# An attention and mixture-of-experts layer on one core: the experts' inner channels as stationary weights, and an empty unit in the planner

## The chip, the core and the metric

The kernel runs on one core of a Trainium2 chip, all in float32. The core has five engines that run beside each other: TensorE (PE in the profile; its weight loads are PEld), VectorE (DVE), ScalarE (ACT), GpSimd (POOL) and SyncE (SP), which here only issues DMAs. The metric is the device time of one execution in microseconds.

## The reference

The input x is 4 x 1024 tokens of 256 channels, treated here as 4096 rows. With xn the layer norm of x, the result is x + attention(xn) + ffn(xn).

The attention part is a causal linear attention of 16 heads of 16 channels, mixed per head with what four memory banks give for the queries. The ffn part is a mixture of experts:

```
scores = softmax(xn @ gate_weight.T)            # 8 experts
cw     = the 2 largest per token, normalized, else 0
g      = silu(xn @ w_gate[e].T) * (xn @ w_up[e].T)   # 176 inner channels
y      = sum over e of cw[e] * (g @ w_down[e].T)
y     += the same with a shared expert of 352 inner channels
```

The change touches the line of g for the eight routed experts.

## The kernel before

Tokens are handled in 8 blocks of 512 (four tiles of 128). A prologue normalizes all blocks, stores xn to DRAM (`xns`), copies x to DRAM (`sums`), and picks two experts for every token. A counting sort then gives every (token, expert) pair a slot: the slots form 71 tiles of 128, each tile belonging to one expert (`owner`). `islot` holds the token of each slot, and `wslot` its weight.

After that come 32 attention rounds, one per token tile (`attention_round`). Each round's list of units names scores (L723), masks (L730), memories (L838, L848 to L867), local attention (L749), its normalization (`back`, L765 to L789) and the state update. `odd_keys(n + 1)` (L710, on ACT) closes round n: it makes `skO`, a masked copy of the next tile's keys `skT`, which the next round's `scores` needs (L723).

Beside the rounds run the projections. `projections(blk)` makes the keys of block blk and the queries of block blk+1 (`project`, L632, then `projected`, L646 and L650, on DVE), and for blocks 3, 4 and 5 the shared expert too. They are divided by weight over the four rounds of the block before blk. Blocks 2, 6 and 7 have no shared part there, so they have at most four pairs of units; with four pairs, the queries stand first and the keys last. For even blocks, `batch_weights` (L672 to L696: a small softmax on DVE and ACT whose result `w5` the batch's rounds need) stands at their end.

The routed experts are a third stream. For slot tile j:

- `fetch_rows(j)`: an indirect DMA by POOL gathers the 128 rows of xn into `xg`.
- `fetch_weights(j)`: SP reads the owner and loads `wgu` (gate and up weights, 256 x 2 x 176) and `wdn` (down weights, 176 x 256, as 88 partitions x 2). Three buffers each.
- `expert_turn(j)`: turns the hidden values of tile j (two transposes, L1071) and the gathered rows of tile j+2 (two transposes, L1075), and copies all four from PSUM (L1077, ACT).
- `expert_hidden(j)`: two matmuls (the two halves of the 256 input channels) with the turned rows as stationary operand and 352 weight columns moving (L1084). Tokens come out on the partitions. tanh (L1089, ACT) and two DVE passes of 176 columns (L1090, L1091) form silu(gate) * up in a tile `hidden`.
- `expert_out(j)`: two matmuls of 88 rows each (L1097), scaled by `wslot` on ACT (L1101).
- `put(j)`: an indirect DMA by POOL adds the rows to `sums` (L1106).

In the stream, `experts()` orders them: hidden(j), put(j-2), out(j-1), turn(j). The order on every engine is the order in which units are recorded. Each unit has a hand-written weight; `mix` interleaves streams by their relative progress in weight, and `split` divides a stream into parts. The experts fill rounds 2 to 29 up to a common level of weight:

```
share = [weight(rounds[n]) + weight(beside[n]) for n in range(first_round, last_round)]
level = max(share)
cap = 1.25 * weight(work) / len(share)
```

where `weight` leaves out units without arguments. All matmul outputs but the scores rotate through four PSUM banks (`bank`), so a unit needs that the fourth unit before it has been read out. In the last rounds the outputs and `sums` are added and stored.

Of the kernel before, what the change touches and what calls it, by code (L numbers as in the profile page):

```python
# [8 lines left out]
FP = mybir.dt.float32  # L9
I32 = mybir.dt.int32  # L10
AF = mybir.ActivationFunctionType
ALU = mybir.AluOpType
AX = mybir.AxisListType

P = 128
# [7 lines left out]
def linear_attention_moe_kernel(  # L23
# [28 lines left out]
    nc = tc.nc  # L52
    T, H = x.shape
# [3 lines left out]
    NC = H // P  # L57
    HC = NH // NC
    NG = HC // 2
    NM = memories.shape[1]  # L60
    D1 = HD + 1
    CW = 32
    FR = E * F
    FT = w_gate.shape[1]
    FS = FT - FR
    NF = -(-FS // P)
    FH = F // 2
    assert FH * 2 == F and FH <= P and NC == 2 and NM == 4
    HID = eg_w1.shape[1]
    NBLK = T // TB  # L70
    NTT = T // P
# [1 line left out]
    NST = 2 * NTT + E - 1  # L73
# [7 lines left out]
    const = ctx.enter_context(tc.tile_pool(name="const", bufs=1))  # L81
# [5 lines left out]
    exw = ctx.enter_context(tc.tile_pool(name="exw", bufs=3))  # L87
    exp = ctx.enter_context(tc.tile_pool(name="exp", bufs=2))
    dram = ctx.enter_context(tc.tile_pool(name="dram", bufs=1, space=bass.MemoryType.DRAM))
# [5 lines left out]
    st = {}  # L95
    def bank(name):
        return ps_r.tile([P, 512], FP, tag="r", name=name)
# [76 lines left out]

    xns = dram.tile([T + P, H], FP, tag="xns", name="xns")
    sums = dram.tile([T + P, H], FP, tag="sums", name="sums")
    ident = const.tile([P, P], FP, tag="ident", name="ident")
    make_identity(nc, ident)
    ones = const.tile([P, P], FP, tag="ones", name="ones")
# [64 lines left out]
    mem = const.tile([P, NC, KM], FP, tag="mem", name="mem")  # L244
    normx = const.tile([P, NC, NM, HC], FP, tag="normx", name="normx")
    alive = const.tile([P, NMN], FP, tag="alive", name="alive")

    hidden = [const.tile([P, FH + P], FP, tag=f"hidden{k}", name=f"hidden{k}") for k in range(2)]
    for t in hidden:
        nc.gpsimd.memset(t[:, F:], 0.0)  # L250
    ungate = const.tile([P, NH], FP, tag="ungate", name="ungate")
    gates = const.tile([P, H], FP, tag="gates", name="gates")

# [780 lines left out]
    def fetch_rows(j):  # L1034
        if j >= NST:
            return
        xg = exp.tile([P, H], FP, tag="xg", name=f"xg_{j}", bufs=3)
        nc.gpsimd.indirect_dma_start(  # L1038
            out=xg,
            out_offset=None,  # L1040
            in_=xns,
            in_offset=bass.IndirectOffsetOnAxis(ap=islot[:, j : j + 1], axis=0),
        )
        st["xg", j] = xg

    def fetch_weights(j):
        if j >= NST:
            return
        e = nc.sync.value_load(owner[0:1, j : j + 1], min_val=0, max_val=(E - 1) * F)
        wgu = exw.tile([P, NC, 2, F], FP, tag="wgu", name=f"wgu_{j}")  # L1050
        for g, w in enumerate((w_gate, w_up)):
            nc.sync.dma_start(
                wgu[:, :, g, :],
                w[:, bass.ds(e, F)].rearrange("(k p) f -> p k f", p=P),
            )
        wdn = exw.tile([FH, 2, H], FP, tag="wdn", name=f"wdn_{j}")
        nc.sync.dma_start(
            wdn, w_down[bass.ds(e, F), :].rearrange("(f p) h -> p f h", p=FH)
        )
        st["weights", j] = wgu, wdn  # L1060

    def expert_turn(j):


        fetch_rows(j + 4)
        fetch_weights(j + 3)
        pt = bank(f"pte_{j}").rearrange("p (f t) -> p f t", t=P)
        lo, hi = (0 if j >= 0 else 2), (4 if j + 2 < NST else 2)
        if j >= 0:
            for f in range(2):  # L1070
                nc.tensor.transpose(pt[:, f, :], hidden[j % 2][:, f * FH : f * FH + P], ident)  # L1071
        if j + 2 < NST:
            xg = st.pop(("xg", j + 2))
            for c in range(NC):
                nc.tensor.transpose(pt[:, 2 + c, :], xg[:, c * P : (c + 1) * P], ident)  # L1075
        dst = exp.tile([P, 4, P], FP, tag="turned", name=f"turned_{j}")
        nc.scalar.copy(dst[:, lo:hi], pt[:, lo:hi])  # L1077
        st["hTe", j], st["xgT", j + 2] = dst[:, 0:2], dst[:, 2:4]

    def expert_hidden(j):  # L1080
        xgT, wgu = st.pop(("xgT", j)), st["weights", j][0]
        ph = bank(f"phe_{j}")
        for k in range(NC):
            nc.tensor.matmul(  # L1084
                ph[:, : 2 * F], xgT[:, k, :], wgu[:, k].rearrange("p g f -> p (g f)"),
                start=(k == 0), stop=(k == NC - 1),
            )
        th = hidden[j % 2][:, :F]
        nc.scalar.activation(th, ph[:, :F], AF.Tanh, scale=0.5)  # L1089
        nc.vector.scalar_tensor_tensor(th, th, 1.0, ph[:, :F], ALU.add, ALU.mult)  # L1090
        nc.vector.scalar_tensor_tensor(th, th, 0.5, ph[:, F : 2 * F], ALU.mult, ALU.mult)  # L1091

    def expert_out(j):
        hT, wdn = st.pop(("hTe", j)), st.pop(("weights", j))[1]
        py = bank(f"pye_{j}")
        for f in range(2):
            nc.tensor.matmul(  # L1097
                py[:, :H], hT[:FH, f, :], wdn[:, f, :], start=(f == 0), stop=(f == 1)
            )
        y = exp.tile([P, H], FP, tag="y", name=f"y_{j}", bufs=3)  # L1100
        nc.scalar.activation(y, py[:, :H], AF.Copy, scale=wslot[:, j : j + 1])  # L1101
        st["y", j] = y
# [25 lines left out]
    def run(units):  # L1128
        for _, f, *args in units:
            f(*args)  # L1130

    def late(pairs):

        units = [pairs[0][0]]
        for (_, b), (a, _) in zip(pairs, pairs[1:]):
            units += [a, b]
        return units + [pairs[-1][1]]

    def keys(blk):
        return [  # L1140
            ((1024, project, blk, wk, c, False), (64, projected, blk, c, False))
            for c in range(NC)
        ]

    def queries(blk):
        return [
            ((1024, project, blk, wq, c, True), (64, projected, blk, c, True))
            for c in range(NC)
        ]

    def shared(blk):
        units = []
        for f in range(NF):
            units += [
                ((1024, shared_gate, blk, f), None),
                ((1024, shared_up, blk, f), (64, shared_hidden, blk, f)),
            ]
        return units
# [11 lines left out]
    def projections(blk):  # L1170

        pairs = keys(blk) + (queries(blk + 1) if blk + 1 < NBLK else [])

        pairs += shared(blk) if 2 < blk < NBLK - 2 else []
        if len(pairs) == 4:
            pairs = pairs[2:] + pairs[:2]
        units = [u for pair in pairs for u in pair]
        if blk % BPB == 0:
            b = blk // BPB
            at = units.index(pairs[3 if len(pairs) > 6 else 1][1]) + 1  # L1180
            units[at:at] = [(64, mean_queries, b)]
            at = units.index(pairs[6][0]) if len(pairs) > 6 else len(units)
            units[at:at] = [(64, batch_weights, b)]
        return [u for u in units if u]

    def attention_round(n):

# [17 lines left out]
        return u  # L1205

    def experts():
        units = [(3000, lambda: None), (256, expert_turn, -2), (256, expert_turn, -1)]
        for j in range(NST + 1):
            if j < NST:  # L1210
                units += [(704, expert_hidden, j)]
            units += [(64, put, j - 2)] if j > 1 else []
            units += [(512, expert_out, j - 1)] if j > 0 else []
            units += [(512, expert_turn, j)] if j < NST else []
        return units + [(64, put, NST - 1)]

    def split(units, parts):
# [41 lines left out]
    for blk in range(NBLK):  # L1259
        rows = slice(blk * TB, (blk + 1) * TB)  # L1260
        nc.sync.dma_start(sums[rows, :], x[rows, :])


    def sorting():
# [13 lines left out]
    start = [u for u in late(first_pairs) if u]  # L1278
    start.insert(9, (64, mean_queries, 0))
    start += [(64, batch_weights, 0), (32, odd_keys, 0)]  # L1280
    run(mix(steps(sorting(), 32, 1000), start))


    rounds = [attention_round(n) for n in range(NTT + 2)]
    beside = [[u for pair in shared(blk) for u in pair if u] for blk in (1, 2)] + [[], []]
    for blk in range(2, NBLK):
        beside += split(projections(blk), NT)
# [7 lines left out]
    lists += [(768, add_slots, batches[-2]), (100, hold, batches[-1])]  # L1295
    lists += [(768, add_slots, batches[-1])]
    lists += [(64, inverted), (10, fetch_rows, 0), (10, fetch_rows, 1), (10, fetch_weights, 0)]
    lists = split(lists, first_round)
    for n in range(first_round):
        run(mix(rounds[n], beside[n], lists[n]))  # L1300
# [4 lines left out]
    def weight(units):  # L1305
        return sum(u[0] for u in units if len(u) > 2)

    work = experts()
    share = [weight(rounds[n]) + weight(beside[n]) for n in range(first_round, last_round)]
    level = max(share)  # L1310
# [4 lines left out]
    for n in range(first_round, last_round):  # L1315
        run(mix(*[u for u in (rounds[n], beside[n], side[n - first_round]) if u]))
# [76 lines left out]
```

## Time and profile before

| | |
|---|---|
| median of three runs | 691.95 us (688.85 to 694.77) |
| the profiled execution | 687.07 us, span 685.4 us, mean granted clock 0.99 |
| busy: PE, PEld, DVE | 646.1, 461.9, 454.8 us |
| busy: ACT, POOL | 267.1, 386.8 us |
| DMA | 81.52 MB, mean 119 GB/s |
| expert matmuls phe (L1084), pye (L1097) | 97.5 and 76.7 us of PE busy time |
| expert gathers (L1038), scatters (L1106) | 70.5 and 113.3 us of POOL busy time |

The profile is of one execution, so a sum is made against its 687.07 us, not against the median. Busy times of PE overlap, since matmuls are pipelined: the start of an instruction against the start of the next one is the cost. Each float32 matmul stands in the trace as two instructions with a weight load each, and a transpose as one. A group's line gives busy time and the mean of one in ns, then the idle time of the engine just before it and what ended it. The profile also lists, for any stretch, the clock that was granted to TensorE.

### The profile page before, as it was taken

What the parts mean: (1) busy time and instruction counts of PE and PEld (TensorE: products, weight loads), DVE (VectorE), ACT (ScalarE), POOL (GpSimd) and SP (SyncE); (2) the same over time, 40 slices, a digit from 0 to 9 for tenths busy, and PEclk for the clock granted to TensorE, in tenths of its full rate; (3) what the DMA queues carried; (4) which work ended last, traced back from release to release, by engine and by line L of the source; (5) the groups of instructions that cost most, each with busy time, mean ns of one, the idle gap of its engine ahead of it and who ended that gap; (6) DMA issues with size and microseconds to landing.
All of it is one profiled execution on the core that took longest, in us unless ns stands there. A gap on an engine that the chain in (4) does not pass through costs nothing.

```text
span 685.4 us, 14244 instructions
## 1 busy us (share of the span) xinstructions
PE 646.1 (94%) x5084; PEld 461.9 (67%) x5084; DVE 454.8 (66%) x1198; ACT 267.1 (39%) x614; POOL 386.8 (56%) x424
## 2 busy tenths in 40 slices
PE   4999999899999899999999999999898999999896
PEld 3874565677777666676776767677676776667475
DVE  6838997666666657565756666666676566777672
ACT  3754644334444343334433333334343444334210
POOL 4300254556776735565565555566666567686575
PEclk9999999999999989999999999999999999999999
DMA  9683000436565623344453433345556466563384
GB/s 302 216 279 93 0 1 2 119 91 160 119 145 127 141 64 84 91 100 94 95 103 88 98 95 92 83 112 125 120 124 142 102 145 139 127 149 75 80 282 154
DMA packets 86483, 81.52 MB, mean 119 GB/s; under 512 B 7549, under 2 KB 84013, under 8 KB 86285
## 3 DMA queue, kind: packets, MB, share of 16 engines
q1 hardware_dynamic: 71085, 60.40, 30.6%
q0 software_dynamic: 13632, 18.62, 16.0%
q10 hardware_dynamic: 1696, 1.58, 0.7%
q8 instruction: 41, 0.67, 0.4%
q14 instruction: 29, 0.24, 0.1%
HBM read 62.62 MB, written 22.15 MB: 124 GB/s over the span
## 4 chain that ended last, share of the span: by engine, by line
PE 78%; DVE 14%; ACT 3%; issue 2%; POOL 1%; DMA 1%; DVEq 0%; ACTq 0%
PE phe L1084 13%; PE pye L1097 9%; PE po L990 6%; PE quad L723 5%; PE psu L953 5%; PE pv L396 4%; PE pg L939 4%; PE pn L749 4%; PE po L994 4%; PE quad L838 4%; PE pk L632 3%; PE pq L632 3%; PE pte L1071 2%; PE pt L892 2%; PE pte L1075 2%
## 5 line engine op out<-in xcount | busy, mean ns | idle before, releaser
L1106 POOL DMA_INDIRECT sums<-y,islot x71 | 113.3, 1596 | 70.3 <-DMA sums<-y,islot 18.8
L1084 PE MATMUL phe<-wgu,turned 128*128 128x352 f32 x276 | 97.5, 476 | 3.0 <-ACT turned L1077 2.2
L1090 DVE SCALAR_TENSOR_TENSOR hidden<-hidden,phe 128x176 f32<-128x176 f32 x71 | 23.8, 335 | 95.5 <-ACT hidden L1089 94.9
L730 DVE TENSOR_TENSOR sT<-quad,causal 128x512 f32<-128x512 f32 x128 | 80.5, 683 | 7.5 <-PE quad L723 7.1
L1038 POOL DMA_INDIRECT xg<-xns,islot x71 | 70.5, 993 | 18.7 <-issue 10.8
L1097 PE MATMUL pye<-wdn,turned 88*128 88x256 f32 x284 | 76.7, 393 | 2.5 <-issue 2.4
L860 POOL TENSOR_TENSOR cg<-coarse,gates 128x256 f32<-128x256 f32 x32 | 24.5, 765 | 95.5 <-DVE h L917 59.0
L1084 PEld LDWEIGHTS phe<-wgu,turned 128*128 128x128 f32 x276 | 48.5, 192 | 25.8 <-issue 6.4
L1097 PEld LDWEIGHTS pye<-wdn,turned 88*128 88x128 f32 x284 | 49.8, 190 | 16.4 <-issue 9.9
L1101 ACT ACTIVATE y<-pye,wslot 128x256 f32<-128x256 f32 x71 | 33.6, 473 | 64.0 <-PE pye L1097 64.0
L878 POOL TENSOR_TENSOR fm<-fm 128x512 f32<-128x512 f32 x32 | 44.1, 1379 | 20.0 <-DVE fm L867 12.4
L1077 ACT COPY turned<-pte 128x512 f32<-128x512 f32 (+1 forms) x71 | 41.1, 578 | 34.2 <-PE pte L1075 32.0
L1089 ACT ACTIVATE hidden<-phe 128x176 f32<-128x176 f32 x71 | 22.5, 317 | 78.6 <-PE phe L1084 76.5
L939 PE MATMUL pg<-xnT,wg 128*128 128x512 f32 (+1 forms) x96 | 45.7, 598 | 1.8 <-DVE loc L783 1.8
L990 PE MATMUL po<-wd,h 128*128 128x256 f32 (+1 forms) x192 | 47.2, 382 | 0.1
L953 PE MATMUL psu<-xnT,wu 128*128 128x512 f32 (+1 forms) x96 | 45.6, 597 | 0.0
L590 POOL TENSOR_TENSOR held<-ones,two 128x213 f32<-128x213 f32 (+1 forms) x22 | 15.3, 702 | 48.7 <-DVE ones L570 48.7
L867 DVE TENSOR_TENSOR fm<-quad,rw 128x512 f32<-128x512 f32 x64 | 42.0, 680 | 0.0
L848 DVE TENSOR_SCALAR rw<-quad 128x80 f32<-128x80 f32 x32 | 7.6, 239 | 49.3 <-PE quad L838 49.3
L990 PEld LDWEIGHTS po<-wd,h 128*128 128x128 f32 (+1 forms) x192 | 35.2, 191 | 6.3 <-ACT oc L902 0.8
L928 DVE SCALAR_TENSOR_TENSOR o<-diff,prob,loc 128x256 f32<-128x256 f32 x32 | 35.5, 1109 | 3.9 <-DVE prob L926 0.5
L749 PE MATMUL pn<-sT,va 128*32 128x128 f32 x1024 | 34.6, 276 | 0.3 <-ACT turned L1077 0.3
(210 smaller groups left out, 1389.0 us busy)
## 6 DMA issues: line engine op xcount, KB each, us to landing
wgu<-in_w_gate_dram SPq DMA_DIRECT2D x71, 176.0 KB
wgu<-in_w_up_dram SPq DMA_DIRECT2D x71, 176.0 KB
wdn<-in_w_down_dram SPq DMA_DIRECT2D x71, 176.0 KB
xns<-x SPq DMA_DIRECT2D x8, 512.0 KB
sums<-in_x_dram SPq DMA_DIRECT2D x8, 512.0 KB
x<-in_x_dram SPq DMA_DIRECT2D x7, 512.0 KB
part<-sums SPq DMA_DIRECT2D x12, 256.0 KB
out_dram<-acc SPq DMA_DIRECT2D x12, 256.0 KB
```

The source lines that it names most:

```text
L632: nc.tensor.matmul(pq, w[:, k, c * P : (c + 1) * P], xnT[:, k, :], start=(k == 0), stop=(k == NC - 1),)
L730: nc.vector.tensor_mul(sT, quad[:, g, :].rearrange("p (c t) -> p c t", t=P), causal[:, None, :].to_broadcast([P, NC * 2, P]),)
L749: nc.tensor.matmul(pn[CW * r : CW * (r + 1), q, :], wide[:, i, first : first + CW], st["sT", h // 2][:, c * 2 + h % 2, :], start=True, sto ...
L867: nc.vector.tensor_mul(fm[:, c].rearrange("p g m (r k) -> p g (m r) k", k=HD), quad[:, :, c * KM + KX + KN : (c + 1) * KM].rearrange("p g ...
L878: nc.gpsimd.tensor_add(fm[:, :, 0:2, :], fm[:, :, 0:2, :], fm[:, :, 2:4, :])
L939: nc.tensor.matmul(pg[:n, :], wg[:, k, f * P : f * P + n], xnT[:, k, :], start=(k == 0), stop=(k == NC - 1),)
L953: nc.tensor.matmul(pu[:n, :], wu[:, k, f * P : f * P + n], xnT[:, k, :], start=(k == 0), stop=(k == NC - 1),)
L990: nc.tensor.matmul(po[:, :H], st["h", blk, f][:k, tok], wd[:k, f, :], start=(f == 0), stop=False)
L1038: nc.gpsimd.indirect_dma_start(out=xg, out_offset=None, in_=xns, in_offset=bass.IndirectOffsetOnAxis(ap=islot[:, j : j + 1], axis=0),)
L1084: nc.tensor.matmul(ph[:, : 2 * F], xgT[:, k, :], wgu[:, k].rearrange("p g f -> p (g f)"), start=(k == 0), stop=(k == NC - 1),)
L1097: nc.tensor.matmul(py[:, :H], hT[:FH, f, :], wdn[:, f, :], start=(f == 0), stop=(f == 1))
L1106: nc.gpsimd.indirect_dma_start(out=sums, out_offset=bass.IndirectOffsetOnAxis(ap=islot[:, j : j + 1], axis=0), in_=st.pop(("y", j)), in_of ...
```

## The change

1. **The operands of the hidden matmuls are swapped.** The gate and up weights (in slices of 128, 128 and 112 columns) are stationary, and the 128 turned tokens move. The inner channels come out on the partitions, ready for the down projection, so the hidden values are not transposed any more. Three output slices of one PSUM bank hold: gate 0 to 111 (with 16 rows not used), gate 112 to 175 above up 112 to 175, and up 0 to 111. The tanh and the first DVE pass run over two slices (256 columns); the product with up is two DVE passes of 128 columns, on 112 and on 64 partitions.
2. **Rearranged up weights.** So that the second slice falls as it does, each expert's up channels are rotated in DRAM: two DMAs at the end of the prologue copy w_up to `ups`, and `fetch_weights` reads `ups`. `wdn` is split 112 + 64 and is loaded as 112 partitions x 2 (224 KB in place of 176, its last 48 rows not used).
3. **Order and weights of the expert stream.** `expert_turn(j)` turns only the gathered rows of tile j and stands before `expert_out`; the stream is hidden(j), put(j-2), turn(j+2), out(j-1). Weights: 768 for hidden (704 before), 256 for turn (512 before). The tiles `hidden` and their memset go.
4. **An idle unit.** For blocks with at most four pairs of projections (2, 6 and 7), an empty unit with a third of their weight is put at the end of the list that is divided over four rounds.

```diff
-        for g, w in enumerate((w_gate, w_up)):
+        for g, w in enumerate((w_gate, ups)):
...
-        wdn = exw.tile([FH, 2, H], FP, tag="wdn", name=f"wdn_{j}")
+        wdn = exw.tile([FA, 2, H], FP, tag="wdn", name=f"wdn_{j}")
...
     def expert_turn(j):
-        fetch_rows(j + 4)
-        fetch_weights(j + 3)
-        pt = bank(f"pte_{j}").rearrange("p (f t) -> p f t", t=P)
-        if j >= 0:
-            for f in range(2):
-                nc.tensor.transpose(pt[:, f, :], hidden[j % 2][:, f * FH : f * FH + P], ident)
...
+        fetch_rows(j + 2)
+        fetch_weights(j + 1)
+        xg = st.pop(("xg", j))
+        for c in range(NC):
+            nc.tensor.transpose(pt[:, c, :], xg[:, c * P : (c + 1) * P], ident)
+        xgT = exp.tile([P, NC, P], FP, tag="turned", name=f"turned_{j}")
+        nc.scalar.copy(xgT, pt[:, :NC])
...
     def expert_hidden(j):
-        for k in range(NC):
-            nc.tensor.matmul(
-                ph[:, : 2 * F], xgT[:, k, :], wgu[:, k].rearrange("p g f -> p (g f)"),
-                start=(k == 0), stop=(k == NC - 1),
-            )
-        th = hidden[j % 2][:, :F]
-        nc.scalar.activation(th, ph[:, :F], AF.Tanh, scale=0.5)
-        nc.vector.scalar_tensor_tensor(th, th, 1.0, ph[:, :F], ALU.add, ALU.mult)
-        nc.vector.scalar_tensor_tensor(th, th, 0.5, ph[:, F : 2 * F], ALU.mult, ALU.mult)
+        for s, cols in enumerate((slice(0, P), slice(FA, FA + P), slice(F + FB, 2 * F))):
+            for k in range(NC):
+                nc.tensor.matmul(
+                    ph[: cols.stop - cols.start, s, :],
+                    wgu[:, k].rearrange("p g f -> p (g f)")[:, cols],
+                    xgT[:, k, :],
+                    start=(k == 0), stop=(k == NC - 1),
+                )
+        th = exp.tile([P, 2, P], FP, tag="th", name=f"the_{j}")
+        nc.scalar.activation(th, ph[:, :2], AF.Tanh, scale=0.5)
+        nc.vector.scalar_tensor_tensor(th, th, 1.0, ph[:, :2], ALU.add, ALU.mult)
+        nc.vector.scalar_tensor_tensor(
+            th[:FA, 0], th[:FA, 0], 0.5, ph[:FA, 2], ALU.mult, ALU.mult
+        )
+        nc.vector.scalar_tensor_tensor(
+            th[:FB, 1], th[:FB, 1], 0.5, ph[FB:, 1], ALU.mult, ALU.mult
+        )
...
-        return [u for u in units if u]
+        units = [u for u in units if u]
+        return units + ([] if len(pairs) > 4 else [(sum(u[0] for u in units) // 3, idle)])
...
-            if j < NST:
-                units += [(704, expert_hidden, j)]
+            units += [(768, expert_hidden, j)] if j < NST else []
             units += [(64, put, j - 2)] if j > 1 else []
+            units += [(256, expert_turn, j + 2)] if j + 2 < NST else []
             units += [(512, expert_out, j - 1)] if j > 0 else []
-            units += [(512, expert_turn, j)] if j < NST else []
...
+    for dst, src in ((slice(FB, F), slice(0, FA)), (slice(0, FB), slice(FA, F))):
+        nc.sync.dma_start(
+            ups.rearrange("h (e f) -> h e f", f=F)[:, :, dst],
+            w_up[:, :FR].rearrange("h (e f) -> h e f", f=F)[:, :, src],
+        )
```

with `FB = P // 2` (64), `FA = F - FB` (112), and `idle` a function that does nothing.

More of the change, by code (lines that the diff above doesn't have):

```diff
@@ L66, in linear_attention_moe_kernel @@
     NF = -(-FS // P)
-    FH = F // 2
-    assert FH * 2 == F and FH <= P and NC == 2 and NM == 4
+    FB = P // 2
+    FA = F - FB
+    assert FA <= P and F >= P and NC == 2 and NM == 4
     HID = eg_w1.shape[1]
@@ L176, in linear_attention_moe_kernel @@
     sums = dram.tile([T + P, H], FP, tag="sums", name="sums")
+    ups = dram.tile([H, FR], FP, tag="ups", name="ups")
     ident = const.tile([P, P], FP, tag="ident", name="ident")
@@ L246, in linear_attention_moe_kernel @@
     alive = const.tile([P, NMN], FP, tag="alive", name="alive")
-    hidden = [const.tile([P, FH + P], FP, tag=f"hidden{k}", name=f"hidden{k}") for k in range(2)]
-    for t in hidden:
-        nc.gpsimd.memset(t[:, F:], 0.0)
     ungate = const.tile([P, NH], FP, tag="ungate", name="ungate")
@@ L1055, in fetch_weights @@
             )
-        wdn = exw.tile([FH, 2, H], FP, tag="wdn", name=f"wdn_{j}")
+        wdn = exw.tile([FA, 2, H], FP, tag="wdn", name=f"wdn_{j}")
         nc.sync.dma_start(
-            wdn, w_down[bass.ds(e, F), :].rearrange("(f p) h -> p f h", p=FH)
+            wdn, w_down[bass.ds(e, 2 * FA), :].rearrange("(f p) h -> p f h", p=FA)
         )
@@ L1062, in expert_turn @@
     def expert_turn(j):
-        fetch_rows(j + 4)
-        fetch_weights(j + 3)
-        pt = bank(f"pte_{j}").rearrange("p (f t) -> p f t", t=P)
-        lo, hi = (0 if j >= 0 else 2), (4 if j + 2 < NST else 2)
-        if j >= 0:
-            for f in range(2):
[L1071 to L1075, printed above, removed]
@@ L1076, in expert_turn @@
-        dst = exp.tile([P, 4, P], FP, tag="turned", name=f"turned_{j}")
-        nc.scalar.copy(dst[:, lo:hi], pt[:, lo:hi])
-        st["hTe", j], st["xgT", j + 2] = dst[:, 0:2], dst[:, 2:4]
+        fetch_rows(j + 2)
+        fetch_weights(j + 1)
+        pt = bank(f"pte_{j}").rearrange("p (c t) -> p c t", t=P)
+        xg = st.pop(("xg", j))
+        for c in range(NC):
+            nc.tensor.transpose(pt[:, c, :], xg[:, c * P : (c + 1) * P], ident)
+        xgT = exp.tile([P, NC, P], FP, tag="turned", name=f"turned_{j}")
@@ L1080, in expert_hidden @@
+        nc.scalar.copy(xgT, pt[:, :NC])
+        st["xgT", j] = xgT
     def expert_hidden(j):
         xgT, wgu = st.pop(("xgT", j)), st["weights", j][0]
-        ph = bank(f"phe_{j}")
-        for k in range(NC):
-            nc.tensor.matmul(
-                ph[:, : 2 * F], xgT[:, k, :], wgu[:, k].rearrange("p g f -> p (g f)"),
-                start=(k == 0), stop=(k == NC - 1),
-            )
-        th = hidden[j % 2][:, :F]
-        nc.scalar.activation(th, ph[:, :F], AF.Tanh, scale=0.5)
@@ L1090, in expert_hidden @@
-        nc.vector.scalar_tensor_tensor(th, th, 1.0, ph[:, :F], ALU.add, ALU.mult)
-        nc.vector.scalar_tensor_tensor(th, th, 0.5, ph[:, F : 2 * F], ALU.mult, ALU.mult)
+        ph = bank(f"phe_{j}").rearrange("p (s t) -> p s t", t=P)
+        for s, cols in enumerate((slice(0, P), slice(FA, FA + P), slice(F + FB, 2 * F))):
[6 more added lines that the diff above has]
+                )
@@ L1093, in expert_out @@
+        th = exp.tile([P, 2, P], FP, tag="th", name=f"the_{j}")
[7 more added lines that the diff above has]
+        )
+        st["hTe", j] = th
     def expert_out(j):
@@ L1095, in expert_out @@
         py = bank(f"pye_{j}")
-        for f in range(2):
+        for f, n in enumerate((FA, FB)):
             nc.tensor.matmul(
-                py[:, :H], hT[:FH, f, :], wdn[:, f, :], start=(f == 0), stop=(f == 1)
+                py[:, :H], hT[:n, f, :], wdn[:n, f, :], start=(f == 0), stop=(f == 1)
             )
@@ L1130, in run, with idle @@
             f(*args)
+    def idle(*_):
+        pass
     def late(pairs):
@@ L1207, in experts @@
     def experts():
-        units = [(3000, lambda: None), (256, expert_turn, -2), (256, expert_turn, -1)]
+        units = [(3000, lambda: None), (256, expert_turn, 0), (256, expert_turn, 1)]
         for j in range(NST + 1):
-            if j < NST:
-                units += [(704, expert_hidden, j)]
+            units += [(768, expert_hidden, j)] if j < NST else []
             units += [(64, put, j - 2)] if j > 1 else []
+            units += [(256, expert_turn, j + 2)] if j + 2 < NST else []
             units += [(512, expert_out, j - 1)] if j > 0 else []
-            units += [(512, expert_turn, j)] if j < NST else []
         return units + [(64, put, NST - 1)]
```

## The prediction

> **What bounds the kernel.** I read the page's head and busy row first, then the chain that ended last.
>
> ```profile
> span 685.4 us, 14244 instructions
> PE 646.1 (94%) x5084; PEld 461.9 (67%) x5084; DVE 454.8 (66%) x1198; ACT 267.1 (39%) x614; POOL 386.8 (56%) x424
> PE 78%; DVE 14%; ACT 3%; issue 2%; POOL 1%; DMA 1%; DVEq 0%; ACTq 0%
> ```
>
> TensorE sets the end: it is 94% busy and 78% of the chain. DVE is second, with 231 us idle, but its 14% says that PE now and then runs up against DVE's order. So TensorE time counts nearly in full, DVE time in part, ACT and DMA time not at all unless they come late. Next, the costliest groups, for durations of what is edited:
>
> ```profile
> L1084 PE MATMUL phe<-wgu,turned 128*128 128x352 f32 x276 | 97.5, 476 | 3.0 <-ACT turned L1077 2.2
> L1090 DVE SCALAR_TENSOR_TENSOR hidden<-hidden,phe 128x176 f32<-128x176 f32 x71 | 23.8, 335 | 95.5 <-ACT hidden L1089 94.9
> L867 DVE TENSOR_TENSOR fm<-quad,rw 128x512 f32<-128x512 f32 x64 | 42.0, 680 | 0.0
> L1077 ACT COPY turned<-pte 128x512 f32<-128x512 f32 (+1 forms) x71 | 41.1, 578 | 34.2 <-PE pte L1075 32.0
> ```
>
> A matmul's 476 ns overlaps with its neighbours, so what an instruction costs is the distance from one start to the next. That is read from the timeline (start, length, engine, line); each f32 matmul stands as two instructions, a transpose as one:
>
> ```profile
> 352.82 0.60 PE L800 MATMUL pk<-ident,skT 128*128 128x128 f32 x4
> 353.26 0.38 PE L1071 MATMUL pte<-ident,hidden 128*128 128x128 f32 x2
> 353.48 0.38 PE L1075 MATMUL pte<-ident,xg 128*128 128x128 f32 x2
> 353.70 1.46 PE L990 MATMUL po<-wd,h 128*128 128x256 f32 x6
> ...
> 355.86 1.35 PE L1084 MATMUL phe<-wgu,turned 128*128 128x352 f32 x4
> 357.05 0.53 PE L672 MATMUL pr<-normx,qr 128*128 128x32 f32 x4
> ...
> 363.86 0.63 PE L771 MATMUL pb<-state,sqT 128*128 128x136 f32 x4
> 364.32 1.35 PE L1084 MATMUL phe<-wgu,turned 128*128 128x352 f32 x4
> ```
>
> Four instructions of 352 moving columns take 357.05 - 355.86 = 1.19 us, 0.297 each; a pair of transposes takes 0.22, 0.11 each; four of 136 columns, each with its own 128x128 load, take 0.46, 0.115 each.
>
> Last, where PE waits. Two large waits stand at the first tiles of blocks 2 and 6 (from two timeline windows and the table of windows, whose column after the five engines is the granted clock):
>
> ```profile
> 236.87 0.81 PE L723 MATMUL quad<-sqT,skO 32*128 32x128 f32 x8 [1.89 <-ACT skO L710]
> 529.55 0.68 DVE L650 SCALAR_TENSOR_TENSOR skT<-pk,ek 128x512 f32<-128x512 f32 x1
> 531.52 0.26 ACT L684 ACTIVATE rel<-rel 128x64 f32<-128x64 f32 x1 [4.12 <-DVE rel L683]
> 531.68 0.49 ACT L710 ACTIVATE skO<-skT,own 128x256 f32<-128x256 f32 x1
> 532.23 0.50 PE L723 MATMUL quad<-sqT,skO 32*128 32x128 f32 x8 [2.90 <-ACT skO L710]
> 236.60:243.40 6.80, 6.53 (x34) 4.30 (x35) 3.74 (x14) 1.59 (x4) 4.85 (x5) 0.50 0.43 75
> 533.60:537.00 3.40, 3.40 (x15) 3.03 (x15) 2.73 (x6) 1.55 (x3) 2.05 (x2) 0.50 0.53 100
> ```
>
> The block's keys (skT) leave DVE only as the block's scores begin; the batch weights (rel) follow on DVE and stand ahead of skO on ACT; PE waits 1.9 and 2.9 us for skO. Right after both waits TensorE's clock is halved, for 6.8 and 3.4 us.
>
> **The expert's matmuls.** Removed per tile of slots: 4 instructions of 352 columns, 4 x 0.297 = 1.19 us, and 2 transposes of the hidden values, 0.22: 1.41. Added: three output groups x two contraction halves x two = 12 instructions of 128 columns. Their spacing isn't in the trace for this shape; the nearest rows give 0.11 (transposes of 128 columns) and 0.115 (136 columns, ordinary f32). I take 0.11: 1.32 us. Gain 0.09 us x 71 tiles = **6 us**. Ends: 0.115 gives 2, 0.107 (352 columns' 0.297 scaled to 128) gives 9. The down projection has two matmuls as before, with 112 and 64 rows in place of 88 and 88: nothing.
>
> The rule against this: the Trainium skill, "TensorE: Matmul & The Clock Gate", sections "LDWEIGHTS (loading the stationary operand)" and "Part 3: Packing small matmuls", says that a load costs its columns over 1.2 (107 ns for 128) and overlaps running matmuls only when the row groups differ. All loads here use all rows. By it, loads add up: before 4 x (107 + 297) + 2 x 217 = 2.05 us, after 12 x 217 = 2.60, so +0.55 x 71 = 39 us slower (an estimate from that page). The trace doesn't agree: at 0.297 and 0.115 a load of 190 ns is plainly under the previous matmul, though rows are the same. I follow the row.
>
> **DVE.** From 335 ns at 176 columns to 680 at 512 is 1.03 ns per column. The two passes of 176 (670 ns) become one of 256 (417) and two of 128 (286 each): 989. That is +0.32 us x 71 = 22.6 us more DVE work. Most lies in idle time: DVE waits 94.9 us just ahead of L1090. What stands behind it on DVE is the normalization (L779 to L783), whose PSUM bank PE wants back, and the masks. Bounds: 0 or slightly below (PE's transposes no longer wait for the hidden values; the result isn't needed before the next tile's down projection), and 22.6 if all is in series. DVE being 14% of the chain points to 14% of 22.6; I take **+3 us**.
>
> **ACT, DMA, POOL.** The copy shrinks from 512 to 256 columns (578 to the 370 ns of a 256-column copy, L1000), the tanh grows by 80 columns (65 ns): 10 us less on an engine that is 39% busy, worth nothing. wdn grows from 176 to 224 KB per tile, 3.4 MB on 81.5: SP waits 306.9 us in all for wdn's buffers to be freed, so loads are ahead of use; uncovered, some 3.4 MB at 119 GB/s, 29 us over 16 engines spread over 71 tiles. The rearranged copy of the up weights is two DMAs of 2048 pieces (448 and 256 bytes). q1's 71085 packets took 30.6% of 16 x 685 us, 47 ns each: 4096 pieces on 16 engines make some 12 us. They queue on SP after the copies to sums, issued by 47 us; SP then waits until 124.9, and slices 5 to 7 of the GB/s row show 0, 1 and 2. First use is at 125.5: hidden with over 50 us to spare, else 12 us once. Row gathers and scatters keep their number and order: expert_turn moves ahead of expert_out, but is one iteration lighter; SP meets wdn's wait for the same down projection.
>
> **The idle unit.** Blocks 2, 6 and 7 have only keys and next queries. A third of their weight as empty work at the end puts all of it in the first three of four rounds; expert tiles fill the fourth. In the new order of instructions block 2's keys and the batch weights come about a round (some 17 us) ahead of skO of tile 8; likewise block 6. So both waits go, 1.9 + 2.9 = 4.8 us, and nothing is left on skO but its own 0.5 us on ACT. Half clock for 6.8 and 3.4 us loses half of that: 5.1. Here a second rule weighs: the same page, section "Why this matters for your kernels", asks for PE gaps over about 3 us before the clock falls back. By it only the second wait, of 2.9, could be the cause, and I could claim 1.7. The trace has the halving after 1.9 us as well (but none after a wait of 2.4 at 490.7), each time at once after the gap; I take **9.9 us** in all, 6.5 by the rule.
>
> **Sum.** On the profiled execution, 687.07 us (span 685.4 and 1.7 around it): -6 - 9.9 + 3 = -13, or 674. The three runs before have their median at 691.95, 4.9 above the profiled one; with the same offset the time is **679 us**.
>
> **Rivals.**
> - DVE becomes the bound: the three passes come due in series, +22.6 in place of 3. 691.95 - 15.9 + 22.6 = 699 us. For it: POOL slows DVE (an o pass of 1.88 us at 490.05 ended in a PE wait of 2.4). Against: a third of DVE's time is idle. Slower than before from 16 of the 22.6 us exposed. Chance 0.09.
> - Weight loads show: by the rule above 691.95 + 39 - 9.9 + 3 = 724 us. It decides from a spacing of 0.125 us on (12 x 0.125 = 1.50, +0.09 x 71 = 6.4, what the rest gains). Against: 0.115 in the trace. Chance 0.06.
> - The waits move rather than go: the denser third of the block or the filled fourth round leaves PE waiting elsewhere, and the clock falls there. 691.95 - 6 + 3 = 689 us. For it: PE is idle 39 us in many small places. Chance 0.11.
>
> The forecast itself has 0.74. About 1% is what a measurement of this kernel tells from no change: faster than 685 has 0.75 (the forecast, and a little of the third rival), within 1% 0.16 (most of the third rival and half of the first, whose 699 lies on the border), slower 0.09. The range, 667 to 690, goes from all bounds at their good end (9 for the matmuls, 2 gained on DVE: 671, and an offset smaller by 4) to the third rival.
>
> **What will show it.** Right: phe with 852 instructions near 276 ns of which 12 take 1.3 us; one pair of transposes per tile; DVE busy near 477 us; no wait of quad for skO over 0.5 us; no half clock near 240 and 530 us; span near 672. Wrong: a spacing over 0.12, new PE waits on DVE lines L779 to L783 or on the hidden passes, or a halved clock at another place.

## The result: 3.4% slower

The changed kernel takes 715.51 us (median of 4 runs, 710.77 to 717.47) against 690.4 for the kernel before in the same comparison: a ratio of 1.0344, with a 95% interval of 1.027 to 1.0417. That is some 24 us more where 13 less were forecast. The median of the kernel before differed between comparisons (686.5 to 690.4), so differences below are taken between ratios; a point is 0.01 of a ratio, 6.9 us. Ratios leave out executions more than 1.5% above the fastest of their kernel: two of e4's four (744.22, the profiled one, and 743.19, against 735.04 and 731.91) and two of e9's 22.

The page of the changed kernel (span 715.8 us), its busy row and chain:

```profile
PE 669.3 (94%) x5510; PEld 484.1 (68%) x5510; DVE 476.5 (67%) x1269; ACT 256.8 (36%) x612; POOL 385.4 (54%) x422
PE 81%; DVE 11%; issue 3%; ACT 3%; DMA 1%; POOL 1%; DVEq 0%; ACTq 0%
```

TensorE still bounds it, with more of the chain than before. DVE rose to 476.5 us, as worked out, and its share of the chain fell. TensorE's costliest groups that were edited (busy us, mean ns, then idle time before them):

```profile
L1083 PE MATMUL phe<-turned,wgu 128*128 128x128 f32 (+1 forms) x852 | 111.3, 281 | 1.5 <-PE pye L1104 0.9
L1104 PE MATMUL pye<-wdn,the 112*128 112x256 f32 (+1 forms) x284 | 91.6, 421 | 5.9 <-ACT turned L1073 2.4
```

The surprise is the last line: pye, the down projection that was costed at nothing, grew from 76.7 us with as many instructions as before. Its timeline, PE and weight loads together (rows of the other engines left out):

```profile
359.49 1.49 PE L1083 MATMUL phe<-turned,wgu 128*128 128x128 f32 x12
360.81 0.60 PE L800 MATMUL pk<-ident,skT 128*128 128x128 f32 x4
...
364.36 1.22 PE L1104 MATMUL pye<-wdn,the 112*128 112x256 f32 x4
364.88 0.29 PEld L1104 LDWEIGHTS pye<-wdn,the 64*128 64x128 f32 x2 [0.33 <-issue]
365.51 0.52 PEld L672 LDWEIGHTS pr<-normx,qr 128*128 128x128 f32 x4 [0.33 <-issue]
365.51 0.63 PE L672 MATMUL pr<-normx,qr 128*128 128x32 f32 x4
```

The 12 hidden matmuls take 360.81 - 359.49 = 1.32 us: exactly the forecast. But four pye instructions take 365.51 - 364.36 = 1.15 us, where four of 256 columns at 0.216 would take 0.86. The weight loads ahead of and behind the 64-row part come late: "issue" of 0.33 us stands before each. Over the whole trace, starts of pye instructions are 0.22 us apart between the two of 112 rows, then mostly 0.308 into the first one of 64 rows, 0.320 between the two of 64 rows, and 0.306 to whatever follows. That sums to 1.154, 0.29 us more per tile of slots, or 20.5 us for 71 (an estimate, and a high one, as the next lines show).

Why that matmul: in the instructions of the built program, matmuls of 88, 96 and 112 rows, and those of 128 rows but for the 32-column ones of L749, carry the array part 128x128; the one of 64 rows carries 64x128, and those of the scores and memories (quad) 32x128. The kernel before already shows what a step from one part to another costs. Here its down projection stands ahead of quad:

```profile
172.82 1.03 PE L1097 MATMUL pye<-wdn,turned 88*128 88x256 f32 x4
173.77 0.86 PE L838 MATMUL quad<-mem,sqT 32*128 32x170 f32 x16
```

That is 0.95 us, where four at 0.216 take 0.86. Over that trace, an 88-row instruction is 0.216 us from its successor, and 0.308 where the successor is quad; a transpose 0.109 and 0.202, a hidden matmul 0.296 and 0.388: 0.09 each time. The Trainium skill has this in "TensorEngine Tiling (Array Packing)", section "Key Properties": changing the tiling mode drains TensorE. It gives no price. Here it is 0.09 us at each border. The 0.10 between the two instructions of 64 rows is no border; the weight load stands late there too, but no run says why. And 23 of the 71 down projections are followed by a matmul of another part in any case, so the step out is not new to them.

The second place is a transposing matmul that stands still (PE, ACT and DVE from the timeline of all engines; some rows left out):

```profile
178.81 0.60 PE L1083 MATMUL phe<-turned,wgu 128*112 128x128 f32 x4
179.45 0.38 ACT L1090 ACTIVATE the<-phe 128x256 f32<-128x256 f32 x1 [0.59 <-PE phe L1083]
179.69 0.63 PE L771 MATMUL pb<-state,sqT 128*128 128x136 f32 x4
179.88 1.45 DVE L928 SCALAR_TENSOR_TENSOR o<-diff,prob,loc 128x256 f32<-128x256 f32 x1
180.15 0.63 PE L818 MATMUL pu<-va,sk 128*128 128x136 f32 x4
181.25 0.41 DVE L1091 SCALAR_TENSOR_TENSOR the<-the,phe 128x256 f32<-128x256 f32 x1
181.69 0.29 DVE L1092 SCALAR_TENSOR_TENSOR the<-the,phe 112x128 f32<-112x128 f32 x1
181.99 0.29 DVE L1095 SCALAR_TENSOR_TENSOR the<-the,phe 64x128 f32<-64x128 f32 x1
182.38 0.41 PE L1071 MATMUL pte<-ident,xg 128*128 128x128 f32 x2 [1.61 <-issue]
```

The profile names no releaser ("issue"), but the last DVE pass ends at 181.99 + 0.29 = 182.28 and PE goes on 0.1 us later. The gathered rows have nothing to do with those passes. Their PSUM bank has: in the built program this turn (of tile 9) takes the bank of the hidden matmul of tile 7, with only two units of PE work between (pb and pu). The banks are not handed round in strict turn: in the built program of the changed kernel the last user of a bank is the fourth unit before in 213 cases and a nearer one in 222. PE waits until tanh and three DVE passes, behind a 1.45 us pass of the attention, have read it out: the wait that the program has just ahead of this turn is for the count that the third pass raises (182.29 in the trace), and for the gathered rows, which had landed by 174.8. And then the clock (table of windows, the clock after the five engines):

```profile
183.40:190.20 6.80, 6.80 (x43) 4.25 (x44) 1.69 (x5) 1.27 (x3) 4.35 (x5) 0.50 0.48 120
```

PE is busy throughout these 6.8 us at half clock, so by estimate the wait of 1.6 us costs another 3.4.

### The profile page after: what moved, and what is told of

Its sections match the earlier page's. It is cut to its first block, busy times and chain, and to the rows that moved or that the text cites. A ratio compares the mean times of both kernels' runs of the same rounds, so it can differ in the third digit from the quotient of the medians.

```text
span 715.8 us, 15184 instructions
## 1 busy us (share of the span) xinstructions
PE 669.3 (94%) x5510; PEld 484.1 (68%) x5510; DVE 476.5 (67%) x1269; ACT 256.8 (36%) x612; POOL 385.4 (54%) x422
## 4 chain that ended last, share of the span: by engine, by line
PE 81%; DVE 11%; issue 3%; ACT 3%; DMA 1%; POOL 1%; DVEq 0%; ACTq 0%
PE phe L1083 14%; PE pye L1104 11%; PE po L990 6%; PE quad L723 5%; PE psu L953 4%; PE pg L939 4%; PE pv L396 4%; PE pn L749 4%; PE po L994 4%; PE quad L838 3%; PE pq L632 3%; PE pk L632 3%; PE pte L1071 2%; PE pt L892 2%; PE pb L765 2%
## 5 line engine op out<-in xcount | busy, mean ns | idle before, releaser
L1083 PE MATMUL phe<-turned,wgu 128*128 128x128 f32 (+1 forms) x852 | 111.3, 281 | 1.5 <-PE pye L1104 0.9
L1083 PEld LDWEIGHTS phe<-turned,wgu 128*128 128x128 f32 (+1 forms) x852 | 101.6, 189 | 13.6 <-issue 9.3
L1091 DVE SCALAR_TENSOR_TENSOR the<-the,phe 128x256 f32<-128x256 f32 x71 | 29.6, 417 | 111.3 <-ACT the L1090 104.3
L1104 PE MATMUL pye<-wdn,the 112*128 112x256 f32 (+1 forms) x284 | 91.6, 421 | 5.9 <-ACT turned L1073 2.4
L730 DVE TENSOR_TENSOR sT<-quad,causal 128x512 f32<-128x512 f32 x128 | 80.5, 682 | 10.1 <-PE quad L723 9.6
L1038 POOL DMA_INDIRECT xg<-xns,islot x71 | 70.2, 989 | 20.5 <-issue 10.9
L1104 PEld LDWEIGHTS pye<-wdn,the 112*128 112x128 f32 (+1 forms) x284 | 43.9, 189 | 39.2 <-issue 30.9
L1090 ACT ACTIVATE the<-phe 128x256 f32<-128x256 f32 x71 | 27.2, 383 | 89.0 <-PE phe L1083 81.8
L990 PE MATMUL po<-wd,h 128*128 128x256 f32 (+1 forms) x192 | 50.1, 399 | 0.9 <-ACT sk L804 0.9
L1073 ACT COPY turned<-pte 128x256 f32<-128x256 f32 x71 | 26.4, 372 | 40.7 <-PE pte L1071 37.0
L1071 PE MATMUL pte<-ident,xg 128*128 128x128 f32 x142 | 28.8, 285 | 7.4 <-PE pu L818 3.7
L749 PE MATMUL pn<-sT,va 128*32 128x128 f32 x1024 | 34.6, 276 | 0.0
L928 DVE SCALAR_TENSOR_TENSOR o<-diff,prob,loc 128x256 f32<-128x256 f32 x32 | 31.0, 969 | 3.9 <-DVE prob L926 0.5
```

The costliest lines, as they stand in the source:

```text
L730: nc.vector.tensor_mul(sT, quad[:, g, :].rearrange("p (c t) -> p c t", t=P), causal[:, None, :].to_broadcast([P, NC * 2, P]),)
L749: nc.tensor.matmul(pn[CW * r : CW * (r + 1), q, :], wide[:, i, first : first + CW], st["sT", h // 2][:, c * 2 + h % 2, :], start=True, sto ...
L990: nc.tensor.matmul(po[:, :H], st["h", blk, f][:k, tok], wd[:k, f, :], start=(f == 0), stop=False)
L1038: nc.gpsimd.indirect_dma_start(out=xg, out_offset=None, in_=xns, in_offset=bass.IndirectOffsetOnAxis(ap=islot[:, j : j + 1], axis=0),)
L1071: nc.tensor.transpose(pt[:, c, :], xg[:, c * P : (c + 1) * P], ident)
L1083: nc.tensor.matmul(ph[: cols.stop - cols.start, s, :], wgu[:, k].rearrange("p g f -> p (g f)")[:, cols], xgT[:, k, :], start=(k == 0), sto ...
```

## The experiments

**e1 and e2: the 64 rows, taken out of the one kernel and put into the other.** e1 is the changed kernel with zeros to 112 rows:

```diff
-            th[:FA, 0], th[:FA, 0], 0.5, ph[:FA, 2], ALU.mult, ALU.mult
+            hid[j % 2][:FA, 0], th[:FA, 0], 0.5, ph[:FA, 2], ALU.mult, ALU.mult
...
-            th[:FB, 1], th[:FB, 1], 0.5, ph[FB:, 1], ALU.mult, ALU.mult
+            hid[j % 2][:FB, 1], th[:FB, 1], 0.5, ph[FB:, 1], ALU.mult, ALU.mult
...
-        for f, n in enumerate((FA, FB)):
+        for f, n in enumerate((FA, FA)):
```

with `hid` two tiles that are zeroed once.

> The changed kernel, but its second down-projection matmul takes 112 rows in place of 64, rows 64 to 111 of the hidden values being zeros of a tile that is kept for that. Nothing else is different, and no instruction is added in the loop. Theory A (the 64-row matmul is built for a 64x128 part of the array, all its neighbours for the whole array, and three weight loads per tile of slots stand open at about 0.1 us each): pye goes back to a spacing of 0.216 us, some 0.28 us x 71 = 20 us less, so about 696 us. Theory B (the loss comes from the order turn before out, and from DVE's third pass): the spacing of pye may mend, but PE waits elsewhere instead, and the time stays above 710 us.

e2 is the kernel before with `for f, n in enumerate((FA, FB))` in its down projection, and `hidden` and `wdn` divided to match.

> The kernel before, with its down projection divided 112 + 64 in place of 88 + 88, wdn loaded as in the changed kernel, nothing else. Theory A: the spacing of pye goes to about 0.31 for three of four instructions, +20 us, about 711 us. Theory B: no change beyond 3 us, about 691 us.

e2 took 707.6 us: ratio 1.0322 (1.0271 to 1.0373), some 22 us, and its starts lie 0.307, 0.320 and 0.306 apart, as in the changed kernel. So the 64 rows alone bring the price (row count and array part come together here, and no run parts them). e1 took 700.17 us, ratio 1.0178 (1.0118 to 1.0237). The pye of e2, then of e1, each followed by the next instruction:

```profile
354.78 1.22 PE L1099 MATMUL pye<-wdn,turned 112*128 112x256 f32 x4
355.93 0.66 PE L802 MATMUL pk<-ident,skT 128*128 128x128 f32 x4
...
359.99 1.03 PE L1107 MATMUL pye<-wdn,hid 112*128 112x256 f32 x4
360.85 0.53 PE L675 MATMUL pr<-normx,qr 128*128 128x32 f32 x4
```

1.15 us in e2, and 0.86 again in e1. Theory A holds, but of its 20 us only 1.66 points, 11 us, came back. Part of what PE saved went elsewhere: in e1's profile PE stands 10.1 us ahead of pte in all (6.6 of it under "issue"), in the changed kernel's 7.4 (1.6), and the mean granted clock of four executions is 0.9855 in e1 (0.981 to 0.99) and 0.988 in the changed kernel, worth some 2 us by estimate.

**e5 and e7: the order.** `expert_out(j-1)` before `expert_turn(j+2)`, on top of e1 (e5) and alone (e7).

```diff
-            units += [(256, expert_turn, j + 2)] if j + 2 < NST else []
             units += [(512, expert_out, j - 1)] if j > 0 else []
+            units += [(256, expert_turn, j + 2)] if j + 2 < NST else []
```

> The kernel with the 112-row down projection (e1), and in the expert stream expert_out(j-1) stands before expert_turn(j+2), as in the kernel before; nothing else. Theory D (what is left of the loss is PE waiting with a turn's transposes for the PSUM bank of the hidden matmul just before, which is free only after tanh and three DVE passes, and the half clock after such waits): one more unit of PE work, 0.86 us, lies between, the waits of 1.3 to 2.3 us ahead of pte go, and the time falls from 700 to about 688 us or less. Rival E (DVE is too slow for the denser rounds, whatever the order): within 4 us of e1, 696 to 704 us.

> The changed kernel with expert_out(j-1) before expert_turn(j+2) and nothing else; its second down-projection matmul keeps its 64 rows. With e1 and e5 this completes a table of two by two. If the two costs are independent: 715 less about 12 for the order, 703 us, of which the 64 rows make 16 (687 with 112 rows). If the 64 rows' price of about 20 us is only paid in full where PE has no other waits: 707 us.

e5 took 687.26 us, ratio 1.0014 (0.9991 to 1.0037); e7 took 701.8 us, ratio 1.0198 (1.0153 to 1.0243). With the changed kernel and e1 this makes a table:

| ratio | turn before out | out before turn |
|---|---|---|
| 64 rows | 1.0344 (changed) | 1.0198 (e7) |
| 112 rows | 1.0178 (e1) | 1.0014 (e5) |

The rows cost 1.66 and 1.84 points (11 and 13 us), the order 1.46 and 1.64 (10 and 11 us). Each of these differences is uncertain by 0.5 to 0.9 points, and within that the two are independent; with both taken out, 0.14 points of the loss are left. Theory D stands: e5 rules out the 696 us and more of rival E. In the built programs, 19 of 71 turns take a hidden matmul's bank in the changed kernel and 20 in e5; what the order changes is how many have only two units of PE work between: 11, and 1 in e5 (in five more, the scores are the third). It is the distance that counts. Part of the order's price is clock: e7's mean granted clock is 0.9932 against the changed kernel's 0.988, e5's 0.9896 against e1's 0.9855, by estimate 3 to 4 us of the 10 or 11.

Why the medians give the rows 13 us at most here and 22 in e2 stays open in part. e7's second expectation, the full price where PE has no other waits, did not come true.

**e3, e4 and e8: the idle unit**, added to the kernel before (e3), removed from the changed kernel (e4) and from e5 (e8). The edit is the last line of `projections`.

> The kernel before with the idle unit alone. Theory of the prediction: the waits of 1.9 and 2.9 us for skO at the first tiles of blocks 2 and 6 go with the half clock after them, about 10 us less, 681 us. Rival C (the waits move: DVE and ACT are as late at some other tile): 688 to 692 us, with a wait of 1.5 us or more and a halved clock at another place.

> The changed kernel without the idle unit. If the idle unit does what the prediction said, the two waits for skO come back and the time rises by up to 10 us, to 725. Rival C: within 4 us of the changed kernel, 712 to 719 us.

> e5 (112 rows, out before turn) without the idle unit. In the kernel before, the idle unit was worth 6 us; in the changed kernel with its own order 24 us. If the 24 came from the waits for the bank in the dense rounds, which the order has removed, the idle unit is worth 6 us or less here: 687 to 694 us. If the dense rounds are slow for another reason, 700 us or more.

e3 took 680.94 us, ratio 0.9913 (0.9878 to 0.9948). The two stretches in which the kernel before stood for skO have their full clock (windows of e3; the third is another stretch):

```profile
234.50:256.60 22.10, 21.87 (x201) 15.86 (x199) 13.45 (x34) 10.27 (x23) 13.43 (x15) 1.00 0.52 118
528.80:551.70 22.90, 22.69 (x206) 17.05 (x205) 13.83 (x38) 10.20 (x23) 16.78 (x17) 1.00 0.63 141
509.30:516.10 6.80, 6.23 (x44) 4.28 (x42) 3.53 (x14) 1.44 (x4) 5.86 (x6) 0.50 0.39 82
```

So the waits go, as forecast; but other waits stand ahead of other half clocks: one of 1.37 us, ended at 199.96, ahead of 3.4 us from 202.1, and this one ahead of 6.8 us from 509.3:

```profile
509.12 0.50 PE L1071 MATMUL pte<-ident,hidden 128*128 128x128 f32 x2 [1.57 <-DVE loc L783]
```

Of the 10 us, 6 remain. The granted clock of all executions says which part failed: its mean is 0.9916 in the nine of e3 and 0.9906 in the fourteen of the kernel before beside them, by estimate 5.8 and 6.4 us lost at half clock. So the 6 us agree with the 4.8 of waiting, and of the 5.1 us of half clock hardly any came.

e4's ratio is 1.0681 (1.0621 to 1.0741). Here the idle unit is worth 3.4 points, 23 us, which neither theory had. The page of e4 shows where (clock by slices), and its list of PE's waits:

```profile
PEclk9999999999888899999999999999888989999999
```

```profile
PE pte L1071 <- issue: 12.8, 9, 1.7
```

Without the idle unit, the rounds ahead of blocks 2 and 6 fall into step: a hidden matmul, pb, pu, and a turn that wants the bank, round after round. 18 turns have only two units between, against 11. Waits of 1.4 to 1.7 us come some 24 us apart, each with 6.8 us of half clock behind it; eight such stretches stand in e4's trace. e8 points to these as the cause: with the other order the idle unit is worth 1.0087 - 1.0014 = 0.73 points, 5 us, about as much as in the kernel before. There the two waits for skO at tiles 8 and 24 stand again, of 3.8 us each.

**e6, e11 and e10: the DVE's time.** One more pass of 176 columns per tile, into a tile that nobody uses, in the kernel before (e6) and in e3 (e11); and e5 without its third pass (e10), which leaves 64 of the 176 hidden channels at zero.

```diff
         nc.vector.scalar_tensor_tensor(th, th, 0.5, ph[:, F : 2 * F], ALU.mult, ALU.mult)
+        extra = exp.tile([P, F], FP, tag="extra", name=f"extra_{j}")
+        nc.vector.scalar_tensor_tensor(extra, th, 0.5, ph[:, F : 2 * F], ALU.mult, ALU.mult)
```

> The kernel before with one more DVE pass of 176 columns per tile of slots (335 ns, close to the 320 ns that the change adds to DVE), reading the hidden matmul's bank into a tile that nobody uses. Rival E: the DVE's extra time is what costs, 8 us or more, 695 us and up. The prediction's term: +3 us, 690 us. In series in full it would be +24 us, 711 us.

> The kernel before with the idle unit (e3) and with e6's extra DVE pass of 335 ns per tile into an unused tile. If DVE's time costs the same whatever else is there: 681 + 6 = 687 us, the time of e5, and the swapped matmuls themselves then give nothing or next to nothing. If it is hidden once the waits at blocks 2 and 6 are gone: 681 to 683 us.

> e5 without the third DVE pass, which is left out: 64 of the 176 hidden channels stay zero. DVE's work per tile is then 417 + 286 = 703 ns, near the 670 of the kernel before. If DVE's extra time is what is left between e5 (687) and the kernel before with the idle unit (681, e3): 680 us or less. If the 12 short matmuls cost more than the removed work, in spite of their spacing: 685 to 688 us.

e6 took 692.81 us, ratio 1.0097 (1.0065 to 1.0129); e11 686.58, ratio 1.0003 (0.9985 to 1.0021), 0.9 points above e3. So 335 ns more per tile, 23.8 us of DVE work, cost 6 to 7 us in the kernel before, whether or not the waits at blocks 2 and 6 are there. In e5 the third pass (286 ns) is worth less: e10 took 685.88 us, ratio 0.999 (0.9966 to 1.0014), 0.24 points or 1.6 us below e5, and the intervals overlap.

**e9: earlier gathers.** `fetch_rows(j + 3)` in place of `j + 2`, with four buffers and one more fetch at the start, on e5.

> e5 with the gathered rows fetched three tiles ahead in place of two (four buffers, one more fetch at the start). In e5 PE waited 5.7 us for gathered rows, once 3.2 us with a half clock of 6.8 us after it. If this is what is left: those waits go, 679 to 683 us, faster than the kernel before. If the last 6 us lie in DVE's third pass (e6), 686 us as in e5.

e9 took 689.05 us, ratio 0.9993 (0.9969 to 1.0017): no difference to e5. In its profile PE's wait for gathered rows fell from 5.7 to 1.7 us, and other waits grew: 5.8 for nT (4.0 in e5), one of 3.3 for y (1.6 in e5). A miss: without the late gathers, PE waited for something else.

**What stays open.** e5 has all of the change's parts, without its two costs, and is 1.0 point, 7 us, slower than e3, which has the idle unit alone. PE's removed work should put it 5 us ahead (below). The third DVE pass explains some 1.6 us, not clear of noise, the gathers none. The mean granted clock (0.9896 in e5, 0.9916 in e3) is worth some 1.4 us by estimate. PE's busy time did fall (638.8 us in e5's profile, 646.3 in e3's), but these two profiles cannot show where the rest goes: e5's is of one of its shortest executions (683.87 us) and e3's of one of its longest (684.37). No run says what it is. The fastest version is e3, ahead of both kernels.

## Why the prediction was wrong, point by point

- **Hidden matmuls: right.** Spacing 0.112 us for 128 weight columns and 0.109 for 112 (0.11 was taken); 12 take 1.32 us. The rule on weight loads, weighed against the row, would have failed here: these loads are hidden. By the spacings the gain is 5 to 6 us of PE's time, but no total shows it: e5 is level with the kernel before though it has the idle unit as well.
- **"With 112 and 64 rows in place of 88 and 88: nothing": the first step that failed.** It is 0.29 us per tile in spacing, 20.5 us; in run time 22 us in e2, 11 to 13 in the changed kernel. The spacing of the 88-row instructions was read as that of any row count. No row of the trace had 64; the 32-row groups (quad) were there, and with them the borders between array parts, but I didn't read what the step into and out of them costs. It was 0.09 us, in the same trace and for the same instruction. The rival "weight loads show" was the right mechanism at the wrong matmul.
- **"PE's transposes no longer wait for the hidden values": the second.** They no longer read them, but may still wait for the same DVE pass through the PSUM bank. The turn was moved closer behind the hidden matmul, and only its queues (SP and POOL) were walked through, not its bank. Price: 1.46 to 1.64 points, 10 to 11 us, where 0 stood.
- **DVE +3 us: too small in the kernel before, not shown wrong after the change.** In the kernel before, an extra pass costs 6 to 7 us; a quarter of it shows, not 14%. With the other order (e5), taking out the third pass, 71 x 286 ns = 20.3 us of DVE work, gives 1.6 us, which agrees with 0 and with 3.
- **The idle unit -9.9 us: right for the waits, wrong for the clock.** The waits for skO at tiles 8 and 24 went (4.8 us), but the clock fell after others, so the 5.1 us for half clock hardly came; -6 us in e3. In the changed kernel's profile a wait of 1.9 us for skO stands at the start of tile 23 instead, with 6.8 us of half clock behind it. This is the rival "the waits move", in part.
- **DMA and the copy of the up weights: right, nothing.** PE's list of waits has no weights in it.

In ratios, from e5 by way of e1: 1.0014 + 0.0164 (order) + 0.0166 (rows) = 1.0344.

## What to carry to other kernels

Before changing the row count of a matmul, look up for which part of the array it will be built, and read from the trace what a step between parts costs: here a lone 64-row matmul between full ones cost more than the zeros that pad it. When a unit is moved in a hand-written order, walk through its PSUM bank as well as its inputs: who held the bank, and how much work of the same engine lies between. And price a short stall by what follows it, for here a wait of 1.6 us on a bound TensorE cost 5 by estimate; but taking one wait away does not take the half clock with it if others are left.

## What was not expected of the hardware

A matmul of 64 rows at the first partition, between two of 112 and 128, had starts 0.306 to 0.320 us apart where 0.216 is usual; one of 88, 96 or 112 rows did not. A step between array parts cost 0.09 us for each shape that shows it (0.216 to 0.308, 0.109 to 0.202, 0.296 to 0.388). TensorE fell to half clock at waits of 1.2 to 2.2 us (and at a few longer ones), in stretches of 3.4 or 6.8 us, but not after every one: of the wait of 2.4 us at 490.7 in the kernel before there is no trace in the clock. The rule of a gap over about 3 us, which the prediction weighed, would have missed all halvings inside the changed kernel's profile (at waits of 1.6, 1.9, 1.3 and 2.2 us) and all eight long ones of e4 (1.4 to 1.7).
